# The decays of even and odd groups in places of their own, and one product of layer 1's output stage on GpSimd

## The chip, the cores and the metric

The kernel runs on one core of a Trainium2 chip. Its time is the device time of one execution in microseconds (us), given as the median of several runs. Engines are named as in the profile: PE (TensorE), DVE (VectorE), ACT (ScalarE), POOL (GpSimd), and SP, whose queue issues all the DMAs. "Lnnn" is a line of the kernel before.

## The reference, cut to what matters

The input x has shape (16, 64, 64, 96): 16 images of 64 x 64 positions with 96 channels, in float32. Two layers are added to it, one after the other.

```python
# layer 0
x = x + conv0(_gn(x))     # upsample x2, 96->384->96 with a quadratic between, low-pass, every second row and column
# layer 1, cut
xz = einsum('bhwc,pc->bhwp', _gn(x), in_proj_w); xc, z = xz[..., :192], xz[..., 192:]
xc = silu(depthwise_conv3x3(xc)); z = silu(z)
xs = [xc by rows, xc by columns, both reversed]            # 4 directions k, 4096 positions, 192 channels d
delta = softplus(...)                                      # from xs
h[l] = exp(delta[l] * A) * h[l-1] + delta[l] * u[l] * B[l] # 16 states a channel, for each k and d
y[l] = sum over states of h[l] * C[l] + u[l] * D
y = the four directions added up, at their places
y = (y - mean(y)) * rsqrt(var(y) + 1e-5) * z               # over the 192 channels
x = x + y @ out_proj_w.T
```

The recurrence over l is the bulk: 16 images x 4 directions x 192 channels x 16 states are 196,608 independent chains of 4096 steps.

## The kernel before, in words

The scan is cut into **units**. An image has 8 steps (two pairs of directions, each in 4 chunks of T = 1024 positions), a step has 6 blocks, a block has 4 values of j: 192 units an image, 3072 in all. A unit n holds two **groups**, e = 1 and e = 0, of 128 rows each (32 channels x 4 states), so an operand of a group is a tile of 128 x 1024 float32. The work of a unit:

- `decay(n, e)` (L785-789): ACT makes exp(A * delta) into a tile `da` in PSUM (L788). A `da` takes two of the eight PSUM banks. The pool `sc_aps` has two places for it, so four banks; the other four are two for the side work (`b_ps`), one for `y` and one for the projection.
- `drive(n)` (L792-795): POOL makes b = (delta * u) * B for both groups at once, 128 x 2048 (L794). It is called two units ahead. Four such tiles exist.
- `recur(n, e)` (L797-805): DVE runs the recurrence as one scan instruction over 1024 positions (L803 forward, L805 reversed), with `da` and `b` as its inputs. For e = 0 the result is written over `da`. For e = 1 it is written over `b` in four units out of five; in every fifth unit (`odd_here`) it too is written over `da`.
- the product with C: for e = 0 on DVE out of PSUM (L972), for e = 1 on POOL in SBUF (L963), or in the `odd_here` units on DVE (L954).
- `keep` (L811): a copy of the last column, the state for the next chunk.
- `read_out(n - 1)` (L827): PE adds up the 4 states by a matmul into `y`.

The order in which every engine meets these instructions is written out by hand (`tc.manual_schedule()`): each engine takes its instructions in the order of the program, and only waits on semaphores move them in time. In a unit the order is: scan of (n, 1); `keep`; decay (n+1, 1); slot 0; POOL's product L963 and drive(n+2); scan of (n, 0); read_out(n-1); slot 1; L972; `keep`; decay (n+1, 0); slot 2. Which of the two PSUM places a decay gets is not written in the code: the pool hands one out as the recorder sees one come free.

The three **slots** carry the side work of the other stages. `front(mi+1)` (layer 0, and layer 1's convolution, of the next image) and `finish(mi-1)` (layer 1's output stage of the image before) are generators; each `yield` ends a slice, and a slot runs at most one slice of them, by a clock of 499 slices to 576 slots an image. `yield HEAVY` counts as two slices. `finish` is only stepped when `front` is through, so it fills the last fifth of each image's scan; the `finish` of the last image runs after the scan by itself.

`finish` goes over an image in 8 tiles of 512 positions. In a tile PE makes the centred y in two parts `yc` (L557, L569), ACT squares them (L566, L584), DVE multiplies them by z (L578, L588), PE adds the squares up (L585, L589), ACT makes the inverse deviation r by a Ln and an Exp (L594, L595), and PE makes the output product `o_ps` (L598). Then

```python
            e_ps = bank([C, TB], "oe_ps")
            ...                                   # L602: three matmuls add the bias and the residual into e_ps
            nc.vector.tensor_mul(r, o_ps, r)      # L603
            yield HEAVY
```

and in the middle of the next tile `end` adds r into `e_ps` by one more matmul (L607), ACT copies it out (L610) and SP stores it. The `bank` tiles of `finish` share the two banks of `b_ps`, and its SBUF tiles (`piece`) share eleven places.

Of the kernel before, what the change touches and what calls it, by code (L numbers as in the profile page):

```python
# [45 lines left out]
F32 = mybir.dt.float32  # L46
# [3 lines left out]
PSUM = bass.MemoryType.PSUM  # L50

C = 96
# [10 lines left out]
T = 1024  # L63
# [3 lines left out]
TB = 512  # L67
# [7 lines left out]
HEAVY = 2  # L75
# [5 lines left out]
def tile_two_blocks(  # L81
# [4 lines left out]
    nc = tc.nc  # L86
# [103 lines left out]
    def bank(shape, name):  # L190
        return banks[-1].tile(shape, F32, name=name, tag="bank")

    def piece(shape, name):
        return b2p.tile(shape, F32, name=name, tag="piece")

    def parts(out, in_, n=4):

        step = L // n
        for i in range(n):
            nc.sync.dma_start(out=out[:, step * i:step * i + step], in_=in_[:, step * i:step * i + step])  # L200
            yield
# [323 lines left out]
    def finish(mi):  # L525

        y_d, xs_d, z_d, x1_d = (image[mi][k] for k in ("y", "xs", "z", "x1"))
        ycol = [b18.tile([128, L], F32, name="ycol0", tag="b18"), b16.tile([64, L], F32, name="ycol1", tag="b16")]
        yield from parts(ycol[0], y_d[1, 0:128, :])
        yield from parts(ycol[1], y_d[1, 128:DI, :], 2)  # L530

        def fetch_y(t):
            cols = slice(TB * t, TB * t + TB)
            y0, u0, yu = piece([128, TB], "y0"), piece([128, TB], "u0"), piece([128, TB], "yu")
            nc.sync.dma_start(out=y0, in_=y_d[0, 0:128, cols])
            nc.sync.dma_start(out=u0, in_=xs_d[0, :, cols])
            nc.sync.dma_start(out=yu[0:64], in_=y_d[0, 128:DI, cols])
            nc.sync.dma_start(out=yu[64:128], in_=xs_d[2, 0:64, cols])
            return y0, u0, yu

        ahead = fetch_y(0)
        for _ in range(2):
            yield HEAVY
        tail = None
        for t in range(8):
            cols = slice(TB * t, TB * t + TB)
            y0, u0, yu = ahead
            z0, z1, xt = piece([128, TB], "z0"), piece([64, TB], "z1"), piece([C, TB], "xt")
            nc.sync.dma_start(out=z0, in_=z_d[0:128, cols])
            nc.sync.dma_start(out=z1, in_=z_d[128:DI, cols])  # L550
            nc.sync.dma_start(out=xt, in_=x1_d[:, cols])
            yc, sq, yz = [], [], []
            for ob, n in ((0, 128), (1, 64)):
                oc = slice(128 * ob, 128 * ob + n)
                y_ps = bank([n, 8, HW], "yc")
                for i, (w, of) in enumerate(((pmat_s[:, 0, oc], y0), (pd_s[:, 0, oc], u0), (pd_s[:, 1, oc], yu))):
                    nc.tensor.matmul(  # L557
                        y_ps, lhsT=w, rhs=of.rearrange("c (h w) -> c h w", w=HW), start=(i == 0), stop=False
                    )
                    if i == 1:  # L560
                        yield
                if tail is not None:
                    tail = next(tail, None) and tail
                if ob == 1:
                    sq.append(piece([128, TB], "sq"))
                    nc.scalar.activation(sq[0], yc[0], AF.Square)  # L566
                yield
                for i in range(2):
                    nc.tensor.matmul(  # L569
                        y_ps.rearrange("c h w -> c w h"), lhsT=pmat_s[0:128 if i == 0 else 64, i, oc],  # L570
                        rhs=ycol[i].rearrange("c (w h) -> c w h", h=HW)[:, :, 8 * t:8 * t + 8],
                        start=False, stop=(i == 1),
                    )
                if tail is not None:
                    tail = next(tail, None) and tail
                if ob == 1:
                    yz.append(piece([128, TB], "yz"))
                    nc.vector.tensor_mul(yz[0], yc[0], z0)  # L578
                yc.append(y_ps.rearrange("c h w -> c (h w)"))
                yield HEAVY  # L580

            v_ps = bank([C, TB], "v_ps")
            sq.append(piece([64, TB], "sq"))
            nc.scalar.activation(sq[1], yc[1], AF.Square)  # L584
            nc.tensor.matmul(v_ps, lhsT=mean_s, rhs=sq[0], start=True, stop=False)  # L585
            yield
            yz.append(piece([64, TB], "yz"))
            nc.vector.tensor_mul(yz[1], yc[1], z1)  # L588
            nc.tensor.matmul(v_ps, lhsT=mean_s[0:64], rhs=sq[1], start=False, stop=True)  # L589
            if t < 7:  # L590
                ahead = fetch_y(t + 1)
            yield
            r = sq[0][0:C]
            nc.scalar.activation(r, v_ps, AF.Ln, bias=eps_n[0:C])  # L594
            nc.scalar.activation(r, r, AF.Exp, scale=-0.5)  # L595
            o_ps = bank([C, TB], "o_ps")
            for i, n in ((0, 128), (1, 64)):
                nc.tensor.matmul(o_ps, lhsT=ow_s[0:n, i, :], rhs=yz[i], start=(i == 0), stop=(i == 1))  # L598
            yield HEAVY
            e_ps = bank([C, TB], "oe_ps")  # L600
            for i, (w, of) in enumerate(((ob_s[:, 0, :], z0), (ob_s[0:64, 1, :], z1), (ident_s[0:C, 0:C], xt))):
                nc.tensor.matmul(e_ps, lhsT=w, rhs=of, start=(i == 0), stop=False)  # L602
            nc.vector.tensor_mul(r, o_ps, r)  # L603
            yield HEAVY

            def end(r, e_ps, cols):
                nc.tensor.matmul(e_ps, lhsT=ident_s[0:C, 0:C], rhs=r, start=False, stop=True)  # L607
                yield True
                o = piece([C, TB], "o")
                nc.scalar.copy(o, e_ps)  # L610
                yield True
                nc.sync.dma_start(out=out[mi, :, cols], in_=o)

            tail = end(r, e_ps, cols)
        for _ in tail:
            yield HEAVY
# [6 lines left out]
    def scan():  # L623


        with ExitStack() as es:
# [142 lines left out]
                    if (what, 0, j) not in bc:  # L769
                        bc[what, 0, j] = fetch_bc(ctxs[0], 0, j, what)  # L770
            banks.append(es.enter_context(tc.tile_pool(name="b_ps", bufs=2, space=PSUM)))
            aps = es.enter_context(tc.tile_pool(name="sc_aps", bufs=2, space=PSUM))
            yps = es.enter_context(tc.tile_pool(name="sc_yps", bufs=1, space=PSUM))
            gps = es.enter_context(tc.tile_pool(name="sc_gps", bufs=1, space=PSUM))

# [2 lines left out]
            def group(n, e):  # L778
                st, bi, _ = units[n]
                v, s0, r = blocks[bi]  # L780
                return 2 * steps[st][1] + r, s0 + e if v < 2 else 4 + e
# [2 lines left out]

            def decay(n, e):  # L785
                k, g = group(n, e)
                da = aps.tile([128, T], F32, name="da")
                nc.scalar.activation(da, deltas[n // NQ, e], AF.Exp, scale=a_s[:, k, g, units[n][2]:units[n][2] + 1])  # L788
                das[n, e] = da

# [121 lines left out]
            for e in range(2):  # L912
                decay(0, e)
            storing, credit = None, 0

            for n, (st, bi, j) in enumerate(units):
                mi, pair, lc = steps[st]
                v, s0, r = blocks[bi]
                m = n // NQ
                if n % per_image == 0:  # L920
                    image[mi]["y"] = dram.tile([2, DI, L], F32, name="y_d")
                    behind_gen.drain()
                    ahead_gen = behind_gen = nothing
                    if mi + 1 < B:
                        ahead_gen = Background(front(mi + 1), SLICES, POS)
                elif n % per_image == 2 and mi > 0:
                    behind_gen = Background(finish(mi - 1), SLICES, POS)
# [28 lines left out]
                if n < last:  # L956
                    decay(n + 1, 1)
# [16 lines left out]
                if n < last:  # L974
                    decay(n + 1, 0)
# [25 lines left out]
    with tc.manual_schedule():  # L1001
        with tc.tile_pool(name="first_ps", bufs=8, space=PSUM) as pool:
            banks.append(pool)
            for _ in front(0):
                pass
            banks.pop()
        scan()
        with tc.tile_pool(name="last_ps", bufs=8, space=PSUM) as pool:
            banks.append(pool)
            for _ in finish(B - 1):  # L1010
                pass
            banks.pop()
# [95 lines left out]
```

## Time and profile before

| | |
|---|---|
| median of 3 runs | 21,318.96 us (21,314.29 to 21,335.73) |
| the profiled execution | 21,326.15 us, of which the span of its instructions 21,324.4 us |
| DVE busy | 19,510.9 us, 91% of the span |
| POOL busy | 19,511.8 us, 91% of the span |
| PE busy | 16,949.4 us, 79% |
| ACT busy | 13,759.8 us, 65% |
| the scan's first and last decay | at 493 us and 21,154 us |
| L603 | 128 instructions, 86.4 us in all, from 2829 us on |

The busy shares are of one profiled execution of the program. "Idle before" in a row is time in which that engine stood still ahead of these instructions, with the instruction whose semaphore ended it. A wait for several semaphores is put down to the one that came last.

### The profile page before, as it was taken

What the parts mean: (1) busy time and instruction counts of PE and PEld (TensorE: products, weight loads), DVE (VectorE), ACT (ScalarE), POOL (GpSimd) and SP (SyncE); (2) the same over time, 40 slices, a digit from 0 to 9 for tenths busy, and PEclk for the clock granted to TensorE, in tenths of its full rate; (3) what the DMA queues carried; (4) which work ended last, traced back from release to release, by engine and by line L of the source; (5) the groups of instructions that cost most, each with busy time, mean ns of one, the idle gap of its engine ahead of it and who ended that gap; (6) DMA issues with size and microseconds to landing.
All of it is one profiled execution on the core that took longest, in us unless ns stands there. A gap on an engine that the chain in (4) does not pass through costs nothing. (4 is left out here: it accounts for less than half of the span.)

```text
span 21324.4 us, 273404 instructions
## 1 busy us (share of the span) xinstructions
PE 16949.4 (79%) x98988; PEld 7262.1 (34%) x98988; DVE 19510.9 (91%) x12983; ACT 13759.8 (65%) x20546; POOL 19511.8 (91%) x5538
## 2 busy tenths in 40 slices
PE   7876788887878778787887888878787787878855
PEld 4423324233343333324333342333433333243221
DVE  0999999999999999999999999999999999999997
ACT  4666666666666666666666666666666666666553
POOL 0999999999999999999999999999999999999996
PEclk8887888888889888898888888888898888988977
DMA  2565565655656566565665656556565665656654
GB/s 83 184 204 188 198 225 191 219 197 197 223 195 226 189 211 210 192 230 184 218 205 197 223 194 219 198 193 223 195 227 188 212 209 193 230 188 216 222 187 140
DMA packets 1855464, 4277.11 MB, mean 201 GB/s; under 512 B 449438, under 2 KB 548670, under 8 KB 1852062
## 3 DMA queue, kind: packets, MB, share of 16 engines
q1 hardware_dynamic: 1854110, 4259.62, 59.5%
q8 instruction: 781, 12.80, 0.3%
q14 instruction: 573, 4.69, 0.1%
HBM read 3380.58 MB, written 878.18 MB: 200 GB/s over the span
## 5 line engine op out<-in xcount | busy, mean ns | idle before, releaser
L794 POOL TENSOR_TENSOR b<-dtu,bt 128x2048 f32<-128x2048 f32 x3072 | 13908.5, 4537 | 593.7 <-DMA dtu<-dtu_d 468.4
L788 ACT ACTIVATE da<-delta,a_s 128x1024 f32<-128x1024 f32 x6144 | 6846.5, 1116 | 3074.8 <-DVE b L972 947.3
L963 POOL TENSOR_TENSOR b<-b,ct 128x1024 f32<-128x1024 f32 x2458 | 5809.4, 2363 | 1052.8 <-DVE new L811 786.2
L827 PE MATMUL y<-b,fold_s 128*32 128x256 f32 x49152 | 3871.0, 438 | 1122.9 <-DVE b L972 663.2
L972 DVE TENSOR_TENSOR b<-da,ct 128x1024 f32<-128x1024 f32 x3072 | 3756.5, 1223 | 91.8
L803 DVE TENSOR_TENSOR_SCAN da<-da,new,b 128x1024 f32<-128x1024 f32 x1383 | 3246.6, 2348 | 206.5 <-ACT da L788 198.8
L805 DVE TENSOR_TENSOR_SCAN da<-da,new,b 128x1024 f32<-128x1024 f32 x1361 | 3194.1, 2347 | 200.8 <-ACT da L788 188.6
L827 PEld LDWEIGHTS y<-b,fold_s 128*32 128x32 f32 x49152 | 1394.5, 119 | 3847.4 <-issue 1492.7
L805 DVE TENSOR_TENSOR_SCAN b<-da,new,b 128x1024 f32<-128x1024 f32 x943 | 2208.1, 2342 | 112.8 <-ACT da L788 81.0
L803 DVE TENSOR_TENSOR_SCAN b<-da,new,b 128x1024 f32<-128x1024 f32 x921 | 2156.3, 2341 | 10.5 <-ACT da L788 9.9
L811 ACT COPY new<-da 128x1 f32<-128x1 f32 x2764 | 432.9, 157 | 2568.8 <-DVE b L972 2178.3
L488 PE MATMUL c_ps<-xgp,wtap_s 96*64 96x512 f32 (+1 forms) x4608 | 1721.4, 632 | 180.4 <-ACT row L506 175.1
L697 PE MATMUL s<-w,ident_s 128*128 128x512 f32 x1530 | 1166.9, 854 | 722.4 <-ACT w L692 618.0
L371 PE MATMUL h_ps<-xu,w1t_s 96*128 96x500 f32 x1920 | 1053.7, 646 | 362.2 <-ACT sd L362 185.5
L383 PE MATMUL o_ps<-w2c_s,hsq 128*100 128x96 f32 x9600 | 1044.3, 267 | 207.3 <-ACT hsq L352 206.9
L805 DVE TENSOR_TENSOR_SCAN da<-da,b 128x1024 f32<-128x1024 f32 x482 | 1103.8, 2290 | 106.7 <-ACT da L788 98.9
L677 PE MATMUL s<-pr,dtw_s 128*128 128x512 f32 x1530 | 937.8, 697 | 302.0 <-ACT delta L703 214.5
L803 DVE TENSOR_TENSOR_SCAN da<-da,b 128x1024 f32<-128x1024 f32 x460 | 1053.5, 2290 | 107.1 <-ACT da L788 106.9
L383 PEld LDWEIGHTS o_ps<-w2c_s,hsq 128*100 128x100 f32 x9600 | 979.0, 179 | 447.8 <-ACT hsq L352 263.2
L820 PE MATMUL y<-y,ident_s 128*128 128x512 f32 x768 | 532.2, 781 | 627.3 <-ACT yt L838 501.7
L697 PE MATMUL s<-e,ident_s 128*128 128x512 f32 x1530 | 1014.5, 752 | 0.0
L488 PEld LDWEIGHTS c_ps<-xgp,wtap_s 96*64 96x64 f32 (+1 forms) x4608 | 582.9, 169 | 1115.4 <-issue 849.2
(143 smaller groups left out, 21887.5 us busy)
## 6 DMA issues: line engine op xcount, KB each, us to landing
dtu<-dtu_d SPq DMA_DIRECT2D x1536, 512.0 KB
delta<-delta_d SPq DMA_DIRECT2D x1536, 512.0 KB
bt<-rows SPq DMA_DIRECT2D x1024, 512.0 KB
ct<-rows SPq DMA_DIRECT2D x1024, 512.0 KB
u<-xs_d SPq DMA_DIRECT2D x893, 256.0 KB
dtu_d<-dtu SPq DMA_DIRECT2D x765, 256.0 KB
delta_d<-delta SPq DMA_DIRECT2D x765, 256.0 KB
xr<-in_x SPq DMA_DIRECT2D x768, 128.0 KB
```

Source lines behind the costliest of these rows:

```text
L371: nc.tensor.matmul(h_ps[j], lhsT=w1t_s[:, 128 * j:128 * (j + 1)], rhs=xu.rearrange("c p q -> c (p q)"), start=True, stop=True,)
L383: nc.tensor.matmul(o_ps[:, p, :], lhsT=hsq[j][:, UPS * p:UPS * (p + 1)], rhs=w2c_s[:, j, :], start=(j == 0), stop=(j == HB - 1),)
L488: nc.tensor.matmul(c_ps[p:p + n], lhsT=wtap_s[:, tap, 128 * i:128 * i + n], rhs=xgp[:, h0:h0 + 8, dx:dx + HW], start=(tap == 0), stop=(tap ...
L677: nc.tensor.matmul(s, lhsT=dtw_s[:, pair, v, :], rhs=pr, start=True, stop=True)
L697: nc.tensor.matmul(s, lhsT=ident_s, rhs=of, start=(k == 0), stop=(k == 3))
L788: nc.scalar.activation(da, deltas[n // NQ, e], AF.Exp, scale=a_s[:, k, g, units[n][2]:units[n][2] + 1])
L794: nc.gpsimd.tensor_mul(b, dtus[n // NQ], bt.unsqueeze(1).to_broadcast([128, 2, T]))
L803: nc.vector.tensor_tensor_scan(out, da, b, before, ALU.mult, ALU.add)
L805: nc.vector.tensor_tensor_scan(out[:, ::-1], da[:, ::-1], b[:, ::-1], before, ALU.mult, ALU.add)
L827: nc.tensor.matmul(y[32 * q:32 * q + 32, e, :], lhsT=fold_s, rhs=b[:, e, QT * q:QT * q + QT], start=(pair == 0 and j == 0 and e == 0), sto ...
L963: nc.gpsimd.tensor_mul(h, h, bc[1, r, j])
L972: nc.vector.tensor_mul(bs[n][:, 0, :], h, bc[1, r, j])
```

## The change

Two edits are made. The product L603 is taken from DVE: ACT copies `o_ps` into a new SBUF tile, and one slice later POOL multiplies that copy by r. And the decays' pool gets one place for each of two tags, `da0` and `da1`, in the place of two for one tag, so that the decays of the groups e = 0 always lie in one pair of banks and those of e = 1 in the other. The number of banks is the same.

```diff
@@ finish
-            nc.vector.tensor_mul(r, o_ps, r)
-            yield HEAVY
+            o = piece([C, TB], "o")
+            nc.scalar.copy(o, o_ps)
+            yield
+            nc.gpsimd.tensor_mul(r, o, r)
+            yield
@@ scan
-            aps = es.enter_context(tc.tile_pool(name="sc_aps", bufs=2, space=PSUM))
+            aps = es.enter_context(tc.tile_pool(name="sc_aps", bufs=1, space=PSUM))
@@ decay
-                da = aps.tile([128, T], F32, name="da")
+                da = aps.tile([128, T], F32, name="da", tag=f"da{e}")
```

As to the instructions: the program loses 128 products on DVE and gains 128 copies on ACT and 128 products on POOL. No DMA is added or moved. In the program before, 527 of the 3072 units have both of their decays in the same PSUM place, one after the other; in the changed one no unit has.

## The prediction

> **What bounds the kernel now.** I read the page's busy shares first: DVE and POOL are both at 91%. Until the first scan at 496 us and after the last at 21,159 us both are nearly idle, so within the scan's 20,660 us each is busy for about 94%, with 1,150 us of standing still. Such a pair needs the next question: who waits for whom? The groups by line and the waits of DVE and POOL answer it.
>
> ```profile
> PE 16949.4 (79%) x98988; PEld 7262.1 (34%) x98988; DVE 19510.9 (91%) x12983; ACT 13759.8 (65%) x20546; POOL 19511.8 (91%) x5538
> ...
> L794 POOL TENSOR_TENSOR b<-dtu,bt 128x2048 f32<-128x2048 f32 x3072 | 13908.5, 4537 | 593.7 <-DMA dtu<-dtu_d 468.4
> L963 POOL TENSOR_TENSOR b<-b,ct 128x1024 f32<-128x1024 f32 x2458 | 5809.4, 2363 | 1052.8 <-DVE new L811 786.2
> ```
> ```profile
> DVE da L803 <- ACT da L788: 305.7, 318, 1.9
> ...
> DVE da L805 <- ACT da L788: 287.4, 251, 4.5
> ...
> DVE b L805 <- ACT da L788: 98.2, 69, 3.8
> ...
> DVE b L805 <- POOL b L794: 29.5, 59, 0.8
> ```
>
> In the waits the columns are total us, times, longest. DVE waits 593 us (569 times, 1.04 us each) for a decay ahead of a scan that writes `da`, and under 60 us for POOL. POOL's idle time before L963 is a wait for DVE's scan. So DVE leads, and ACT's decays hold it up. ACT is at 65%, so it is not short of time: the decays start late. A timeline shows why (start, duration, engine; in brackets the idle time before):
>
> ```profile
> 9020.33 2.28 DVE L805 TENSOR_TENSOR_SCAN b<-da,b 128x1024 f32<-128x1024 f32 x1
> ...
> 9022.64 2.15 ACT L788 ACTIVATE da<-delta,a_s 128x1024 f32<-128x1024 f32 x2 [0.44 <-DVE b L805]
> ...
> 9023.79 2.30 DVE L805 TENSOR_TENSOR_SCAN da<-da,b 128x1024 f32<-128x1024 f32 x1 [1.00 <-ACT da L788]
> ```
>
> ACT idles until the scan of (n, 1) ends, and only then makes the decay for (n, 0), which DVE needs at once: one decay (1.12 us) lies bare between two scans. That is a unit whose two decays share a place. Joining the scans of the trace with the places in the program: the 527 such units have 558 us of idle time before the second scan, 1.06 each; the other 2,545 have 32 us in all. Where the places differ, the decay of (n, 0) needs only the previous unit's L972 and copy, and runs under the scan of (n, 1), 2.34 us long.
>
> **The Trainium skill.** GPSIMD Engine Reference, "Specifications": GpSimd has no access to PSUM, which is why the product needs a copy; no POOL row here reads a PSUM tile. The same page, "Elementwise — side-by-side cycle accounting", gives 4497 ns for a two-input float32 operation of 2048 columns; the trace has 4537 for L794. SBUF — State Buffer, "Who interferes with whom": a DVE instruction with at most one SBUF input does not contend with GpSimd, one with two does. The trace agrees: L972 (one) takes 1223 ns beside a busy POOL, while `nb` L237, 96x1 with two SBUF inputs, takes 3614. So another POOL product should lengthen no scan. PSUM — Partial Sum Buffer, "PSUM bank collisions raise a hardware error": two engines must not be on a bank at once. Here the state's copy on ACT waits for DVE's L972 on the same tile (2,178 us, 1,437 times); with separate places that copy stays the decay's last release, and there is still a scan to cover it.
>
> **Part 1, the places.** It removes no instruction. 527 x 1.06 = 558 us of DVE's waits go. What replaces them is the 0.012 us a unit of the others (527 x 0.012 = 6 us). The decay of (n+1, 1), which sometimes could start early, now always waits for the scan (n, 1) (2.34 us) or L954 (1.22 us), but has the scan (n, 0) and L972 (3.6 us) as cover; most units already run so, and their waits before the first scan are 149 us in 2,545. If ACT is late with side work this cover fails; I bound that at 60 us.
>
> **Part 2, the product.** DVE loses 128 x 0.675 = 86 us and 29 us of idle before it. ACT gains 128 copies at 0.575 us (L610 is the same shape out of PSUM): 74 us. In the stretches of `finish` ACT is busy for 56 to 64%, so these hide; bare they would cost 74. POOL gains 128 products of 96x512. From L794 and L963 a column costs (4537-2363)/1024 = 2.12 ns on top of 189 ns: 189 + 512 x 2.12 = 1.28 us each, 163 us; half an L963 (1.18) is the lower end, 1.4 the upper. In POOL's queue each stands ahead of L963 or after a drive, so all b tiles behind it come later, unless POOL was idle there. It waits for ACT's copy, one slice earlier (some 2.6 us) and thus done. PE's L607 now waits for POOL; behind it in PE's queue stand the next tile's matmuls and L827. No DMA is added; `xt`'s load waits for another place among the eleven, long read: nothing. After the scan, L603 to L607 had 4.7 us (21,197.8 to 21,202.5), enough for copy and product; only the last tile pays, some 1.5 us.
>
> **How much of it reaches the end** is decided by POOL's idle time in the same stretch, since POOL has 19,512 + 163 = 19,675 us to do. The windows of one image (idle is 100 minus POOL's busy column) beside the waits for a decay before `da` scans in each:
>
> ```profile
> 2500.00:2600.00 100.00, 81.42 (x451) 26.78 (x451) 92.72 (x65) 73.73 (x101) 88.02 (x25) 0.89 0.64 198
> ...
> 2800.00:2900.00 100.00, 94.36 (x414) 30.63 (x417) 94.18 (x73) 63.54 (x97) 98.15 (x30) 0.99 0.71 234
> 2900.00:3000.00 100.00, 92.03 (x392) 29.71 (x388) 97.53 (x65) 58.04 (x81) 99.97 (x30) 0.93 0.71 234
> 3000.00:3100.00 100.00, 89.17 (x390) 28.88 (x383) 98.83 (x61) 60.33 (x77) 97.50 (x29) 0.91 0.65 219
> ```
>
> From 1800 to 2800, in hundreds: waits 4.3, 4.9, 2.3, 4.0, 4.1, 3.4, 3.4, 3.0, 5.0, 4.7; idle 10.4, 3.2, 6.7, 4.4, 4.9, 2.4, 3.5, 12.0, 9.4, 11.1. The smaller of each pair add up to 36.4 us. From 2800 on `finish` runs and POOL is full: it adds 3, 3 and 2 products (3.8, 3.8, 2.6) to 1.9, 0 and 2.5 us of idle, a loss of 2.0, 3.8 and 0.1. Net 30.5 us. This image's waits (42.3) are above the mean, 593/16 = 37.1: scaled, 36.4 x 37.1/42.3 - 5.9 = 26 an image, 416 in 16. The same minimum over the whole trace gives 408 in stretches of 100 us and 310 in stretches of 50. The stretch stands for how far POOL may lag and catch up, which is about a unit (6.9 us); that speaks for shorter ones. I take 360: 21,326 - 360 = 20,966 against the profiled execution, which is 7 us over the median; from the median, **20,960 us**.
>
> **The rivals.**
> - DVE stays the leader and POOL follows without loss: 558 + 86 + 29 = 673 less, 20,650. For it: where neither waits (3600:3700 has DVE 99.4 and POOL 99.8 busy) both run nearly full. Against: POOL is then left 1,150 - 163 - 673 = 314 us of idle in all, and `finish` has none.
> - POOL takes over: a DVE freed of its waits meets POOL behind almost everywhere. In stretches of 40 us the minimum is 275; with half of that lost to queueing, 140 less, 21,180. For it: in 8 of the 13 windows POOL idles under 5%. It would show as waits of DVE for L794.
> - Slower: POOL lags by up to a unit in `finish`, so L607 holds PE's queue (90% busy there) while POOL works off L963 and a drive ahead of the product (6.9 us), and with it `yc`, ACT's squares and the decays behind them. 120 tiles run beside the scan. Part 1 brings some 450 us without part 2; so the end is later than before if a tile costs over 450/120 = 3.8 us. The product's lag less L607's two slices of distance (5.2 us) is about 1.7 + 1.3 = 3 us, of which PE can catch up most; with 5 us a tile the time is 21,319 - 450 + 600 = 21,470.
> - The places bring nothing: the wait only moves to the first scan. Then part 2 alone remains, 5.9 x 15 = 90 slower: 21,410.
>
> **Numbers.** Chances: my forecast 0.58, DVE leads on 0.13, POOL takes over 0.19, L607 0.06, places without effect 0.04; of the takeover 0.02 and of L607 0.01 fall within 0.2%. From 20,760 (short of the full gain) to 21,220 the range takes in the forecast, most of the takeover case and the 60 to 74 us of unknown costs. A measurement of this kernel can tell about 0.2% (43 us) from no change: faster 0.88, same 0.03, slower 0.09.
>
> **What would show it.** Right: the idle time before `da` scans by ACT falls from 593 to under 60 us; POOL's busy share rises to some 93.8%, DVE's to 92.6%; POOL's product has 128 rows of 1.28 us; L963's wait for DVE halves. Waits of DVE for POOL's `b` rise to some 200 us. Wrong: waits for decays stay or move to the `b` scans; waits for POOL of over 400 us; PE's L607 waiting over 400 us, with the `finish` stretches longer by more than 10 us.

## The result, and the profile after

The changed kernel takes 21,196.08 us (median of 4 runs, 21,178.67 to 21,196.55) against 21,320.87 before (4 runs). The ratio is 0.9939 with a 95% interval of 0.9921 to 0.9956: 125 us faster, where 360 were forecast. The time lies inside the forecast range and the direction is right, but the gain is a third of the forecast. The kernel before was measured again beside each set of experiments, with medians from 21,312 to 21,326 us, so a difference between kernels of two sets is good to some 15 us.

In the changed kernel every line from L607 on stands 3 lower: L788 is now L791, L803 and L805 are L806 and L808, L811 is L814, L963 is L966, L972 is L975. The page's busy shares come first, of the profiled execution (span 21,176.9 us):

```profile
PE 16898.3 (80%) x98988; PEld 7211.1 (34%) x98988; DVE 19518.9 (92%) x12855; ACT 13845.0 (65%) x20674; POOL 19658.7 (93%) x5666
```

POOL is busy for 147 us more than before. But DVE, from which 86 us of work were taken, is busy for 8 us **more** too. The groups by line and the waits of DVE say why (groups: busy, mean ns of one, idle before; waits: total, times, longest). The first row of the two for L237 is of the kernel before, all others are of the changed one:

```profile
L237 DVE TENSOR_TENSOR nb<-nmean,rg 96x1 f32<-96x1 f32 x32 | 115.6, 3614 | 303.4 <-ACT rg L234 295.4 <-ACT new L811 8.1
L237 DVE TENSOR_TENSOR nb<-nmean,rg 96x1 f32<-96x1 f32 x32 | 200.1, 6253 | 302.7 <-ACT rg L234 295.1 <-ACT new L814 7.6
```
```profile
L606 POOL TENSOR_TENSOR sq<-o,sq 96x512 f32<-96x512 f32 x128 | 162.9, 1273 | 149.8 <-ACT o L604 102.2 <-DMA z<-z_d 47.6
```
```profile
DVE b L808 <- POOL b L797: 153.4, 196, 2.2
...
DVE da L808 <- ACT da L791: 131.4, 132, 4.0
DVE b L808 <- ACT da L791: 96.5, 69, 3.7
DVE da L806 <- ACT da L791: 94.6, 89, 2.1
```

The product of 96x1, L237, rose from 115.6 to 200.1 us in 32 instructions. The waits for a decay ahead of scans that write `da` fell from 593 to 226 us; they were to fall under 60. POOL's wait for DVE ahead of L963 was to halve and fell from 786 to 616 us. All waits of DVE's scans for POOL rose from 58 to 222 us.

A sum over DVE accounts for the profiled execution, 147 us shorter than the one before: waits for decays before `da` scans -367, L603 with its idle time -115, waits for POOL +164, L237 +85, waits of the other side products (L578, L588 and the projection's dtu) +69. That is -164; the rest is small change in other rows.

The stretch of the first `finish` beside the scan is from L603's or L606's first instruction to its last: 2829 to 3077 us before, 2801 to 3058 after. Before and after (us, then the busy time and the instructions of PE, PEld, DVE, ACT and POOL, then the granted clock and the DMAs):

```profile
2829.00:3077.00 248.00, 230.82 (x979) 74.72 (x977) 242.85 (x167) 149.91 (x209) 245.47 (x71) 0.96 0.69 228
2801.00:3058.00 257.00, 230.08 (x988) 72.94 (x986) 244.50 (x160) 153.63 (x214) 257.00 (x80) 0.96 0.68 225
```

POOL is busy for 257.00 of 257.00 us; in the other 14 stretches of the changed kernel it is idle for 1.5 us at most. Over the first 13 such stretches the mean length went from 250.1 to 258.5 us.

### The profile page after: what moved, and what is told of

Its sections match the earlier page's. It is cut to its first block, busy times and chain, and to the rows that moved or that the text cites. A ratio compares the mean times of both kernels' runs of the same rounds, so it can differ in the third digit from the quotient of the medians.

```text
span 21176.9 us, 273757 instructions
## 1 busy us (share of the span) xinstructions
PE 16898.3 (80%) x98988; PEld 7211.1 (34%) x98988; DVE 19518.9 (92%) x12855; ACT 13845.0 (65%) x20674; POOL 19658.7 (93%) x5666
## 5 line engine op out<-in xcount | busy, mean ns | idle before, releaser
L791 ACT ACTIVATE da<-delta,a_s 128x1024 f32<-128x1024 f32 x6144 | 6855.4, 1117 | 2509.7 <-DVE b L975 868.7
L966 POOL TENSOR_TENSOR b<-b,ct 128x1024 f32<-128x1024 f32 x2458 | 5806.8, 2362 | 783.1 <-DVE new L814 616.1
L975 DVE TENSOR_TENSOR b<-da,ct 128x1024 f32<-128x1024 f32 x3072 | 3757.3, 1223 | 93.4
L806 DVE TENSOR_TENSOR_SCAN da<-da,new,b 128x1024 f32<-128x1024 f32 x1383 | 3245.4, 2347 | 73.5 <-ACT da L791 56.3
L808 DVE TENSOR_TENSOR_SCAN da<-da,new,b 128x1024 f32<-128x1024 f32 x1361 | 3193.7, 2347 | 122.5 <-ACT da L791 88.2
L808 DVE TENSOR_TENSOR_SCAN b<-da,new,b 128x1024 f32<-128x1024 f32 x943 | 2210.1, 2344 | 240.2 <-POOL b L797 151.2
L806 DVE TENSOR_TENSOR_SCAN b<-da,new,b 128x1024 f32<-128x1024 f32 x921 | 2156.4, 2341 | 8.0 <-ACT da L791 7.5
L814 ACT COPY new<-da 128x1 f32<-128x1 f32 x2764 | 433.0, 157 | 2586.5 <-DVE b L975 2210.6
L808 DVE TENSOR_TENSOR_SCAN da<-da,b 128x1024 f32<-128x1024 f32 x482 | 1103.5, 2289 | 53.1 <-ACT da L791 43.2
L806 DVE TENSOR_TENSOR_SCAN da<-da,b 128x1024 f32<-128x1024 f32 x460 | 1053.1, 2289 | 45.0 <-ACT da L791 38.3
```

The costliest lines, as they stand in the source:

```text
L806: nc.vector.tensor_tensor_scan(out, da, b, before, ALU.mult, ALU.add)
L808: nc.vector.tensor_tensor_scan(out[:, ::-1], da[:, ::-1], b[:, ::-1], before, ALU.mult, ALU.add)
L966: nc.gpsimd.tensor_mul(h, h, bc[1, r, j])
L975: nc.vector.tensor_mul(bs[n][:, 0, :], h, bc[1, r, j])
```

## The experiments

**Each edit alone** (e1, e2). e1 has the two hunks of the pool, e2 the hunk of `finish`.

> The places alone; the product stays on DVE. Theory T (DVE still leads; of the 558 us that the shared places cost, about 210 come back because ACT itself is late with its side work, and some 85 because the product nb L237, which has two SBUF inputs, is kept out by a GpSimd that now has hardly a pause): the output stage goes back to its old length, 9 us less in each of 15 images than with both edits, so about 21,196 - 135 = 21,060. Rival P (GpSimd has become the bound everywhere): only its 163 us of products go, 21,030, and then DVE's waits for b fall evenly over the image and not in the output stage alone. Rival S (the places bring nothing, the product all of the gain): 21,320. In the trace T wants waits for decays before da scans of some 220 us and L237 still near 200 us.

> The product on GpSimd alone; the decays keep their two common places. Theory T: the output stage is GpSimd-bound, so 8 products of 1.27 us lengthen each of 15 by about 6 to 9 us and DVE's saved 86 us buy nothing: 21,320 + 90 to 135 = 21,410 to 21,455, L237 unchanged at some 116 us, waits for decays before da scans unchanged at 590 us. Rival S: faster by DVE's 86 to 115 us, 21,210.

The places alone: 21,097.31 us, ratio 0.9896 (0.9881 to 0.9911). The product alone: 21,400.59 us, ratio 1.0039 (1.0025 to 1.0053). So the change is a gain of 220 us and a loss of 83 in one kernel; together that is 137, and 125 were measured. The forecast for e1 was 37 us too low, that for e2 9 us too high at its lower end. In the profiled executions e1 is 227 us shorter than the kernel before, and DVE's rows come to nearly that: 363 us less of waits for decays before `da` scans, 79 more in L237, 47 more of waits for POOL. For e1, the waits of DVE and the row of L237:

```profile
DVE da L805 <- ACT da L788: 131.2, 121, 4.8
...
DVE b L805 <- ACT da L788: 101.9, 69, 3.7
DVE da L803 <- ACT da L788: 98.7, 92, 2.3
DVE b L805 <- POOL b L794: 55.9, 102, 0.9
```
```profile
L237 DVE TENSOR_TENSOR nb<-nmean,rg 96x1 f32<-96x1 f32 x32 | 194.9, 6089 | 303.8 <-ACT rg L234 296.2 <-ACT new L811 7.6
```

230 us of decay waits stay without the product too, and L237 is at 195 us without it. Both belong to the places. In e2, without the places, the waits are at 649 us, not at 590 as expected, and L237 at 116, as before. The `finish` stretches have 250.1 us on the mean in e1 and 258.5 in e2: the 8.4 us belong to the product.

**What keeps the decays late** (e8, e4). Going unit by unit through both traces: of the 527 units whose decays had shared a place (558 us of idle time before the second scan), 178 still wait for a decay there in the changed kernel, 175 us. What ended ACT's own idle time ahead of the late decay parts these units into three kinds, already in the kernel before:

| ACT ahead of the second decay, kernel before | units | DVE's wait before | after |
|---|---|---|---|
| stands idle until the scan (or L954) of its own unit has ended | 472 | 452 us | 77 us |
| has no pause: it is still at other work | 40 | 54 us | 50 us |
| stands idle until the load of `delta` has landed | 14 | 51 us | 46 us |

The waits of one unit more and those of under 0.15 us are left out. Only in the first kind was the shared place the reason that ended last. The other two kinds, 105 us, could gain next to nothing from a place of their own. Here is a unit of the third kind, ACT and DVE in the kernel before and ACT in the changed one:

```profile
4080.88 2.15 ACT L788 ACTIVATE da<-delta,a_s 128x1024 f32<-128x1024 f32 x2 [4.97 <-DMA delta<-delta_d]
4082.03 2.36 DVE L805 TENSOR_TENSOR_SCAN da<-da,new,b 128x1024 f32<-128x1024 f32 x1 [3.87 <-ACT da L788]
4039.59 2.15 ACT L791 ACTIVATE da<-delta,a_s 128x1024 f32<-128x1024 f32 x2 [4.83 <-DMA delta<-delta_d]
```

Why this load is late was not looked into. Of all 226 us of waits before `da` scans in the changed kernel, 52 us (21 waits) stand behind a late `delta`, and the other 174 behind work that ACT had ahead of the decay without a pause. The timelines of ACT and of DVE in the changed kernel show one of the latter:

```profile
3806.74 1.11 ACT L473 COPY col<-row 128x512 f32<-128x512 f32 x1
3807.76 0.14 ACT L814 COPY new<-da 128x1 f32<-128x1 f32 x1
3807.94 2.15 ACT L791 ACTIVATE da<-delta,a_s 128x1024 f32<-128x1024 f32 x2
```
```profile
3806.03 2.28 DVE L808 TENSOR_TENSOR_SCAN b<-da,b 128x1024 f32<-128x1024 f32 x1
3808.34 0.15 DVE L814 COPY new<-b 128x1 f32<-128x1 f32 x1
3809.09 2.30 DVE L808 TENSOR_TENSOR_SCAN da<-da,b 128x1024 f32<-128x1024 f32 x1 [0.59 <-ACT da L791]
```

But for the copy of the state L814 (0.14 us, on ACT itself) the place has been free since L975 ended at 3806.1. ACT takes its queue in order, though, and there stand two steps of the projection (L694 and L695, up to 3806.8) and the turning copy L473. The decay starts at 3807.94 and DVE waits 0.59 us. e8 takes this copy away nearly whole:

```diff
-                    col.rearrange("c (w h) -> c w h", w=HW)[:, :, 8 * t:8 * t + 8],
-                    row.rearrange("c (h w) -> c w h", w=HW),
+                    col.rearrange("c (w h) -> c w h", w=HW)[:, :, 8 * t:8 * t + 1],
+                    row.rearrange("c (h w) -> c w h", w=HW)[:, :, 0:1],
```

> Both edits; of the copy that turns the convolution's rows into columns (L473 on ACT, 1.09 us, 192 times) seven eighths are left out, and two DMAs fill the tile in their place. Theory T (what is left of the waits for decays is ACT's own side work right ahead of them): of the 226 us of waits before da scans the 43 us in 61 units that have this copy right ahead of the decay go, and with them 40 to 70 us of the time: 21,125 to 21,155. Rival Q (the decays are late because delta lands late, or because ACT is short of time in all): waits at these units stay, or all waits fall in proportion to the 180 us of ACT's work taken away (1.3% of it, 3 us); 21,190.

21,158.12 us, 38 less than with both edits and 3 over the range, and the waits before `da` scans fell from 226 to 184 (this kernel has its lines two further down):

```profile
DVE da L808 <- ACT da L793: 95.5, 92, 2.1
DVE da L810 <- ACT da L793: 88.2, 73, 3.4
```

In the changed kernel 43 us of the waits, in 61 units, stood right behind this copy, and these are gone; those behind a late `delta` are not (44 us). How much of the 42 us reaches the end is less sure: 38 us by the medians, but only 23 between the two profiled executions, where the waits of the `b` scans for decays rose by 26 us. e4 tried to clear the way by order instead:

```diff
                 if n >= 1:
                     read_out(n - 1)
-                slot(1)
...
                 if n < last:
                     decay(n + 1, 0)
+                slot(1)
```

> Both edits, and the second of a unit's three slots of side work moved from before the product L975 to after the decay of (n+1, 0), so that no side work of that slot stands ahead of that decay in ACT's queue. Theory T (what is left of the waits for decays is side work ahead of them on ACT): waits before da scans fall from 226 to under 60 us and the time by 100 to 170 us, to 21,030 to 21,100. Rival Q (these decays are late because their delta arrives late by DMA, or because ACT is short of time in all): waits for decays stay above 180 us and the time within 30 us of 21,196. Rival P: the waits fall, but waits for b rise by as much, 21,180.

This expectation was wrong: 21,318.34 us, 122 more than with both edits. The waits it aimed at did fall, to 120 us, of which 47 stand behind work of ACT and 72 behind a late `delta`: each theory had a part of them. But as many and more came up elsewhere:

```profile
DVE dtu L705 <- PE s L700: 481.5, 224, 140.0
...
DVE yz L578 <- ACT sq L566: 191.9, 52, 27.4
DVE b L808 <- ACT new L814: 179.8, 114, 2.7
DVE da L808 <- ACT da L791: 68.6, 40, 4.9
```

Two slots back to back make the next thing late: the scans of e = 1 wait 180 us for ACT's copy of the state, and DVE's side products wait 143 us more for PE's projection and 44 more for ACT's squares. The two runs together say that side work on ACT delays most of the late decays and a late `delta` the rest, but not that moving the side work a place along is free. e10, below, is a third try.

**The product of two SBUF tiles** (e3, e5, e6). Why should a 96x1 product take 6 us? DVE and POOL in the changed kernel, around the longest of them:

```profile
2444.48 12.32 DVE L237 TENSOR_TENSOR nb<-nmean,rg 96x1 f32<-96x1 f32 x1 [0.22 <-ACT rg L234]
2456.73 2.28 DVE L808 TENSOR_TENSOR_SCAN da<-da,b 128x1024 f32<-128x1024 f32 x1
```
```profile
2441.04 4.53 POOL L797 TENSOR_TENSOR b<-dtu,bt 128x2048 f32<-128x2048 f32 x1
2445.51 2.37 POOL L966 TENSOR_TENSOR b<-b,ct 128x1024 f32<-128x1024 f32 x1
2447.82 8.96 POOL L797 TENSOR_TENSOR b<-dtu,bt 128x2048 f32<-128x2048 f32 x2
```

It starts at 2444.48, while POOL is in a drive, and ends at 2456.80. POOL's run of four instructions ends at 2456.78. The product did not wait for one GpSimd instruction but until POOL had nothing more to do; POOL's next instruction comes only after a wait of 13.17 us for DVE. The same product takes 0.155 us where POOL is idle (at 39 and 312 us). All 30 products of the changed kernel that meet a busy POOL end within 0.02 us of a POOL instruction behind which POOL stands idle for 2.5 us or more. So a product lasts until POOL's next pause, and where POOL has lost a pause it lasts longer. POOL's share of busy time alone does not tell: in e2 it does the work of the changed kernel, and L237 takes 116 us. In e3 ACT makes it, on the changed kernel; in e5 on the kernel before:

```diff
-        nc.vector.tensor_mul(nb, nmean, rg)
+        nc.scalar.activation(nb, nmean, AF.Identity, scale=rg)
```

> Both edits, and the product nb (96x1, L237) made by ACT with a scale in the place of DVE's product of two SBUF tiles. Theory T: the 200 us of L237 leave DVE; as DVE leads outside the output stage nearly all of it is gained, 21,196 - 150 to 200 = 21,000 to 21,045. Rival P (GpSimd is the bound everywhere): DVE's freed time turns into waits for b, 21,190, with waits for b up from 221 to some 400 us.

> The kernel before, with only nb (96x1) made by ACT in the place of DVE's product of two SBUF tiles. Theory T (a DVE instruction with two SBUF inputs stands until GpSimd's queue runs dry, and DVE leads): L237's 116 us leave DVE; since GpSimd is then seldom drained, the next such instruction, L260, stands longer (in the run with both edits it went from 38 to 80 us), so 60 to 110 us are gained: 21,210 to 21,260. Rival N (L237's length is only where the profile books a wait that DVE would have anyway): no change, 21,320, with other waits of DVE up by 116 us.

e3: 21,023.97 us, 172 less than with both edits. e5: 21,196.51, ratio 0.9947 (0.9932 to 0.9962), 116 less than the runs of before beside it: the 116 us of L237 came off the end whole. On ACT the product takes 0.28 us. The expectation for e5 counted on the other instruction with two SBUF inputs, L260, becoming longer; there it hardly did (41.9 us), and the time lies 13 us under the range. In e3 it did:

```profile
L260 DVE TENSOR_TENSOR lin<-lin,ident_s 96x96 f32<-96x96 f32 x16 | 79.8, 4989 | 0.0
```

That is 79.8 us in 16 instructions, 38.1 in the changed kernel. e6 removes both, from the places alone:

```diff
-        nc.vector.tensor_add(lin, lin, ident_s[0:C, 0:C])
+        nc.gpsimd.tensor_add(lin, lin, ident_s[0:C, 0:C])
```

> The places, with the product left on DVE, nb made by ACT and the sum lin (96x96, L260) made by GpSimd, so that DVE has no instruction with two SBUF inputs left in the scan. Theory T: from the places alone (21,097) another 150 to 195 us for L237 and 38 for L260, less a few for the six us of work that GpSimd gains: 20,865 to 20,920. Rival P (GpSimd is the bound): 21,050, with waits for b up by 150 us.

20,849.92 us, ratio 0.9784 (0.9768 to 0.9801), 247 less than the places alone and 15 under the range; L237 and L260 took 233 us in e1. No version that was run is clearly faster, and it beats both kernels.

```profile
PE 16843.6 (81%) x98988; PEld 7209.5 (35%) x98988; DVE 19339.7 (93%) x12935; ACT 13789.3 (66%) x20578; POOL 19505.5 (94%) x5554
```

POOL is at 94% here and DVE's waits for it have hardly grown from e1 (56.2 us before the reversed `b` scans, 55.9 there). So it was not the amount of POOL's work that held the gain down outside `finish`, but the two DVE instructions that stood until POOL paused.

**The product's cost: POOL's time or PE's wait?** (e9, e11). In the changed kernel the idle time of PE and its weight loads behind POOL's product, ahead of L610, is 457 us, 141 times, one of the two signs of the forecast's third rival (the other, stretches of `finish` longer by over 10 us, is not there: 8.4).

```profile
  POOL sq L606: 456.8, 141
```

e9 takes the wait away and leaves POOL's work: L610 adds in ACT's copy, and the product is made for nothing.

```diff
-                nc.tensor.matmul(e_ps, lhsT=ident_s[0:C, 0:C], rhs=r, start=False, stop=True)
+                nc.tensor.matmul(e_ps, lhsT=ident_s[0:C, 0:C], rhs=o, start=False, stop=True)
```

> Both edits, but the matmul L610 takes ACT's copy and not GpSimd's product, so PE no longer waits for GpSimd in the output stage; the product is still made and is not used. Theory T (the output stage is longer because GpSimd has 8 products more to do in it): PE's 457 us of waits for the product go and the time stays within 30 us of 21,196; the output stage still takes 257 us with GpSimd full. Rival R (PE's queue, held by L610, makes the output stage longer): it goes back to 248 us and the time to 21,060 to 21,110.

21,187.21 us, 9 less than with both edits. PE's wait for the product is gone, and the same stretch as above has not moved:

```profile
2801.00:3058.00 257.00, 235.84 (x1007) 75.16 (x1006) 244.53 (x160) 154.73 (x215) 257.00 (x80) 0.95 0.67 224
```

The `finish` stretches have 258.5 us on the mean, as with both edits. So PE's wait is a real wait and costs next to nothing. POOL is busy for the whole stretch with and without it, so POOL's own time is what makes the output stage longer.

> Both edits, with nb made by ACT and lin by GpSimd: the version of e6 plus the product on GpSimd. Theory T (the product costs GpSimd's time in the output stage, whatever DVE does elsewhere): 83 to 100 us over e6, 20,935 to 20,950; against the run with nb alone moved (21,024) this takes the 80 us of L260 away. Rival: with DVE freed, GpSimd has no idle time left anywhere and the product costs its full 163 us, 21,010.

e11 (e6 and the product on POOL): 20,929.00 us, 79 more than e6. This is 6 us under the range. The product costs 79, 83 and 99 us on three kernels (against e6, before and e1), and not its 163 us. Fifteen stretches, each some 8 us longer, would come to more than that; where DVE makes up the rest was not traced.

**A finer turning copy** (e10): e6 with L473 cut into two halves, one slice apart.

```diff
-                    if tap == 3 and turned is not None:
-                        turn(*turned)
+                    if tap in (3, 5) and turned is not None:
+                        turn(*turned, halves_of=(0,) if tap == 3 else (4,))
```

> The version of e6 (places, nb on ACT, lin on GpSimd, product on DVE; 20,850), with ACT's turning copy of 1.09 us split into two halves, one slice apart. All of the work is done. Theory T (a decay is late by the length of the ACT work right ahead of it): the waits before da scans fall from 222 by 20 to 43 us and the time by as much, 20,805 to 20,830. Against it: ACT has 192 instructions more, some 0.2 us each (38 us), and the second half meets another decay; then 20,850 or a little above.

20,850.69 us, the same as e6. The waits before `da` scans fell from 222 to 186, those before the `b` scans of L808 rose from 104 to 120, and ACT is busy for 31 us more with the copies (0.638 us each, 384 times, against 1.09, 192 times). The time does not change; what spends the gain again was not shown beyond these two figures.

## Why the prediction was wrong, point by point

**The mechanism of the places was right.** No other edit touched the decays in e1, and the waits before `da` scans fell by 363 us there (593 to 230).

**The step that failed** is the sum of part 1. It was "527 x 1.06 = 558 us of DVE's waits go. What replaces them is the 0.012 us a unit of the others", with 60 us as the bound on a late ACT. The places bring 220 us (e1), where the forecast carried 450 for them. In e1 193 us of the 558 stay in these units, L237 costs 79 us more and the waits for POOL 47 more; that leaves 239. The forecast had allowed for waits for POOL; the first two of these terms it lacked.

- 1.06 us is the mean over all 527 units, and 0.012 us came from the units that did not share a place and was carried over to those that did. But in 54 of the 527 the shared place was not what ended the wait: ACT was at other work or waited for `delta`, and 97 of those 105 us are still there in the changed kernel. In the other 472 the place hid a second reason: in about a quarter of them the decay would have been late in any case, nearly always behind ACT's side work, 77 us in all. A wait shows only the reason that ends last. The second reason could be read in the forecast's own example, in rows of that timeline that it does not show. In the timeline of ACT in the kernel before, right ahead of the two decays at 9022.64, stand

```profile
9021.04 1.10 ACT L473 COPY col<-row 128x512 f32<-128x512 f32 x1
9022.05 0.15 ACT L811 COPY new<-da 128x1 f32<-128x1 f32 x1
```

  so that in this order of ACT's queue, even with a place of its own, the decay could not have started before 9022.2, and of the 1.00 us of waiting some 0.6 would have stayed. (In the changed kernel the instructions have moved against each other, and this scan does not wait.)
- L237 was quoted as evidence ("takes 3614") for the rule that two SBUF inputs contend, and then the rule was applied to the new product alone. The product L237 itself, which is on DVE's path, was left at its old cost. It rose by 79 us in e1. The forecast named DVE the leader and POOL the one that catches up; that the leader's own instruction waits for POOL to run out of work, and so becomes dearer as POOL loses its pauses, is the term that it lacked.

**The discount was for the wrong reason, and its size was luck.** The forecast brought 558 down to some 450 with the minimum of POOL's idle time and DVE's waits in each stretch. DVE's losses to POOL in e1 have about that size, 47 us of scans waiting for `b` and 79 us in L237. But they do not come from POOL's work being too much for the stretch: the 79 us are a few products that wait for a pause, and e6, which takes them off DVE, gains 247 us more while POOL does the same work. Only in `finish`, where POOL has no idle time, does its work set the pace: there lie 128 of the 222 us for which DVE's scans wait for POOL in the changed kernel, against 18 of 58 before and 25 of 105 in e1.

**Part 2 was right.** 1.28 us a product was forecast and 1.273 measured; 5.9 us an image, 90 in all, was forecast, and 83 (e2) to 99 (both against e1) measured. The reason given holds: POOL is full in `finish`, and L603's saving on DVE bought nothing there. What ACT's 128 copies (0.573 us each) cost by themselves no run separates from the product. The waits of L610 at 457 us were named as a sign of the third rival; the sign came and the rival did not (e9).

**The rivals.** "POOL takes over" gave 21,180 and so came near the measured time, but for another reason: the waits for POOL are 222 us in all, as the forecast itself had, not over 400, and they lie mostly in `finish`. "DVE stays the leader" is nearest to what happened outside `finish`; what it lacked are the decay waits that stay and L237. "The places bring nothing" fell with e1.

## What to carry to other kernels

A wait tells of the reason that ended last. So before the waits of a whole class of units are counted as a gain, part them by what the late instruction's own engine was doing until then: idle for the reason that the edit removes, at other work, or idle for something else. Only the first kind can gain, and there what stands right ahead in the queue is the wait that comes next. When an edit makes an engine busier, reprice every instruction of other engines that contends with it, tiny ones first, if they stand on the leading engine's path. And cost two edits apart: here one was worth 220 us and the other cost 83, and without the second the kernel is faster than with both.

## What was not expected of the hardware

SBUF — State Buffer, "Summary: rules for kernel authors", in the Trainium skill, says that when DVE has two SBUF inputs and GpSimd reads SBUF, the second of the two to issue blocks until the first finishes. Here DVE's product with two SBUF inputs blocked through four POOL instructions, three of which began after it, and ended 0.02 us after POOL's last (2456.80 and 2456.78): 12.32 us against 0.155 alone. The measurement decides for this case: it waited for a pause of POOL, not for the end of one instruction. This is what 30 of 30 such products did in the changed kernel, but only 24 of 30 in the kernel before: six, of 2.3 us each, ended with a POOL instruction that the next one followed without a pause, and so did three of L260's sums in each of the two kernels. So a pause is not the whole rule, and what let those through stays open.
